# A graph network's second layer: one gather in sixty-four issued row by row by ScalarE

## The chip, the cores and the metric

The kernel runs on one core of a Trainium2 chip. A core has five engines that run their own instruction streams and meet at semaphores: TensorE (PE) multiplies matrices, VectorE (DVE) and ScalarE (ACT) do element work, GpSimd (POOL) does element work and also issues indirect transfers, and SyncE (SP) issues plain transfers. ScalarE can issue plain transfers too. The metric is the time of one execution on the device in microseconds (us), as the median of several runs.

## The reference

The graph has 12,500 nodes with 128 features and 400,000 edges, sorted by destination. Two layers follow each other. The first one (an edge network and a node network, each of two small matrix products) is not touched by the change. The second one, which is, computes

```python
# h = relu(layernorm(x)); 8 relations; W is 8 x 128 x 128, b is 8 x 128
H = jnp.einsum('ni,rio->rno', h, W)
msg = (H[etype, src] + b[etype]) * norm      # one row of 128 floats per edge
out = jax.ops.segment_sum(msg, dst, num_segments=h.shape[0])
x = x + relu(out)
```

So for each of the 400,000 edges one row of 512 bytes is fetched from a table with 12,500 x 8 rows, multiplied by the edge's weight, and added to the row of the edge's destination.

## The kernel before

**Tiling.** The edges are cut into tiles of 128 (`P`), eight tiles (`CT`) into a chunk of 1,024 edges, three chunks (`SC`) into a span. There are 391 chunks (`NC`) with 3,128 tiles. Within a chunk, the eight edges at one partition are neighbours in the sorted order, so that nearly all of the eight have the same destination.

**First layer.** A loop over the chunks fetches for each edge 32 floats of its source node by eight indirect transfers a chunk (line 358), runs the edge and node networks, and sums into windows of nodes. After each span it also computes the node rows of the second layer's table `tab_h` (8 relations x 128 floats per node, bias included). Beside the loop a generator, `prepare`, is advanced by one step per chunk. It turns indices and weights into the layouts that the second layer wants: it writes source times 8 plus type to a table `hidx_d` in HBM and loads it back, transposed, into `hidx_sb` (a column of 128 row numbers per tile). It has some 120 steps, and the loop has 390 turns.

**Second layer.** `layer1_once` is a loop over the chunks, fully unrolled. For one chunk:

- GpSimd issues eight indirect gathers (line 950). Each reads a column of `hidx_sb` and brings 128 rows of `tab_h` to the 128 partitions of `hg`, one slot of a tile of 8 x 128 floats. There are five buffers of `hg`.
- VectorE does this twice, for the two destinations that a partition can have (q = 0, 1): multiply `hg` by weights into `v` in PSUM (line 957), and sum `v` over the eight slots into `sm` (line 961).
- ScalarE casts `sm` to `hm` (line 964). This is its only instruction per chunk.
- One turn later (`sum_up`, called between the multiply and the sum of the next chunk) VectorE takes the rounding remainder (line 919), builds two one-hot matrices (line 921), and TensorE sums by destination into `acc` (line 924).
- Once per span SyncE reads the span's first node into a register (line 939), loads the window of nodes (lines 931 and 943), VectorE adds (lines 792 and 796), and SyncE writes back (lines 794 and 797).

**Order.** In the first layer the order of each engine's instructions is held to that of the source. The second layer stands in a conditional block; there the framework's scheduler orders each engine's stream. It also puts all semaphore waits in: all plain transfers, of SyncE and ScalarE together, take turns on eight completion semaphores, and each waits until the transfer before it on its semaphore has landed. The indirect transfers have eight others.

Of the kernel before, what the change touches and what calls it, by code (L numbers as in the profile page):

```python
# [8 lines left out]
F32 = mybir.dt.float32  # L9
F32R = mybir.dt.float32r  # L10
BF16 = mybir.dt.bfloat16
I32 = mybir.dt.int32
AF = mybir.ActivationFunctionType
OP = mybir.AluOpType
AX = mybir.AxisListType
ENG = mybir.EngineType
# [3 lines left out]
P = 128  # L20
D = 128
DE = 64
R = 8
N = 12500
# [5 lines left out]
CT = 8  # L30
# [4 lines left out]
NC = -(-E // CE)  # L35
# [8 lines left out]
T0 = 12 * CT  # L44
QT = 25 * 32
QS = 11
NONE = 16384

@with_exitstack
def gnn_kernel(  # L50
# [34 lines left out]
    nc = tc.nc  # L85
# [18 lines left out]
    const = ctx.enter_context(tc.tile_pool(name="const", bufs=1))  # L104
# [11 lines left out]
    span_d = dram.tile([1, NSP], F32, name="span_d")  # L116
    dst_d, hidx_d, ew_d = (dram.tile([NTP, P], F32, name=f"{name}_d") for name in ("dst", "hidx", "ew"))
    odd_d = dram.tile([1, P], F32, name="odd_d")


    ident = const.tile([P, P], F32, name="ident")
# [18 lines left out]
    hidx_sb = const.tile([P, NTP], I32, name="hidx_sb")  # L140
# [389 lines left out]
    with tc.tile_pool(name="e0", bufs=2) as pool, \  # L530
# [23 lines left out]
        def prepare():  # L554

            nc.sync.dma_start(w_f.rearrange("i (r o) -> i r o", r=R), w.rearrange("r i o -> i r o"))
            yield
            nc.sync.dma_start(b_f, b.to_broadcast([P, R * D]))
            yield
            for g in range(0, NTP, QT):  # L560
                m = min(QT, NTP - g)
                cols = slice(g, g + m)
                for given, table in ((dst_t, dst_d), (et, hidx_d), (ew, ew_d)):
                    raw = pool.tile([P, QT], F32, name="raw")
                    nc.sync.dma_start(raw[:, :m] if given is ew else raw[:, :m].bitcast(I32),
                                      given[:, cols])
                    yield
                    if given is dst_t:
                        nc.vector.tensor_copy(raw[:, :m], raw[:, :m].bitcast(I32))
                    elif given is et:  # L570
                        nc.vector.scalar_tensor_tensor(raw[:, :m], src_sb[:, cols], float(R),
                                                       raw[:, :m].bitcast(I32),
                                                       op0=OP.mult, op1=OP.add)
                    tr = pool.tile([P, QT], F32, name="tr")
                    nc.vector.transpose(tr[:, :m], raw[:, :m])
                    rows = table[cols, :].rearrange("(q r) (a j) -> a r q j", r=32, j=32)
                    for a in range(4):
                        nc.sync.dma_start(
                            rows[a], tr[32 * a:32 * a + 32, :m].rearrange("r (q j) -> r q j", j=32))
                    yield  # L580
            odd = pool.tile([P, NSP // QS], F32, name="odd", bufs=1)
            for i, s in enumerate(range(0, NSP, QS)):
                cols = slice(s * ST, (s + QS) * ST)
                hidx = pool.tile([P, QS * ST], F32, name="hidx")
                for table, to in ((dst_d, rel_t[:, cols]), (hidx_d, hidx), (ew_d, ew_sb[:, cols])):
                    nc.sync.dma_start(to.rearrange("p (c k) -> p c k", k=CT),
                                      table[cols, :].rearrange("(c t) (q k) -> (t q) c k",
                                                               t=CT, k=CT))
                    yield
                nc.vector.tensor_copy(hidx_sb[:, cols], hidx)  # L590
                rel = rel_t[:, cols]
                nc.vector.tensor_sub(rel.rearrange("p (s t) -> p s t", t=ST),
                                     rel.rearrange("p (s t) -> p s t", t=ST),
                                     base[:, s:s + QS, None].to_broadcast([P, QS, ST]))
                yield
                rel = rel.rearrange("p (c k) -> p c k", k=CT)
                off = []
                for k in (0, CT - 1):
                    o = pool.tile([P, QS * SC, CT], F32, name="off")
                    nc.vector.tensor_sub(o, rel,  # L600
                                         rel[:, :, k:k + 1].to_broadcast([P, QS * SC, CT]))
                    off.append(o)
                nc.vector.tensor_mul(off[0], off[0], off[1])
                nc.vector.tensor_mul(off[0], off[0], off[0])
                nc.vector.tensor_reduce(odd[:, i:i + 1], off[0].rearrange("p c k -> p (c k)"),
                                        AX.X, OP.max)
                yield
            most = pool.tile([P, 1], F32, name="most", bufs=1)
            nc.vector.tensor_reduce(most, odd, AX.X, OP.max)
            nc.sync.dma_start(odd_d.rearrange("o p -> p o"), most)  # L610
            yield
            odds = pool.tile([1, P], F32, name="odds", bufs=1)
            nc.sync.dma_start(odds, odd_d)
            yield
            nc.vector.tensor_reduce(vm[:, 1:2], odds, AX.X, OP.max)
            worst = pool.tile([1, 1], F32, name="worst", bufs=1)
            nc.vector.tensor_reduce(worst, vm, AX.X, OP.max)
            nc.vector.tensor_scalar(bad, worst, 0.0, None, op0=OP.is_gt)
            yield
            nc.sync.dma_start(x1_d[NP:NP + P, :], zeros[:, 0, :])  # L620
            yield from zero(zeros, agg_d)

        class Span:
# [16 lines left out]
            def end(self, left):  # L640

                a2 = add0(pool, self.aw, self.acc, P)
                if left:
                    nc.sync.dma_start(agg0_d[ds(self.row, P), :], a2)
                banks = ("u", "u", "u") if left else ("pre", "pm0", "pm1")
                steps = rows_h(pool, psum, self.row, self.x0, a2, banks)
                active.append(steps)
                if left:
                    node_step()
                else:  # L650
                    next(steps)
                    next(steps)
# [237 lines left out]
    def layer1_once():  # L890
# [3 lines left out]
        with tc.tile_pool(name="e1", bufs=2) as pool, \  # L894
# [33 lines left out]
            def write():  # L928
# [2 lines left out]
                nc.sync.dma_start(aw, agg_d[ds(row, P), :])  # L931
                return lambda: add_out(pool, aw, xw, (acc[:, 0:D], acc[:, D:2 * D]), row)

            for c in range(NC):
                s, k = divmod(c, SC)
                if k == 0:
                    if s % WS == 0:
                        w_p = weights(s)
                    row = nc.values_load(
                        span[0:1, s:s + 1], engines=[ENG.SP], min_val=0, max_val=N - 1,  # L940
                        skip_runtime_bounds_check_because="a span's least dst is a node")
                    xw = pool.tile([P, D], F32, name="xw1", bufs=3)
                    nc.sync.dma_start(xw, x1_d[ds(row, P), :])
                    acc = psum.tile([P, 512], F32, name="acc1", bufs=3)
                    sums_of.append((acc, row, xw))
                    if s:
                        end = write()
                hg = pool.tile([P, CT, D], F32, name="hg8", bufs=5)
                for t in range(c * CT, c * CT + CT):
                    nc.gpsimd.indirect_dma_start(  # L950
                        out=hg[:, t - c * CT, :], out_offset=None, in_=tab_hr,
                        in_offset=bass.IndirectOffsetOnAxis(ap=hidx_sb[:, t:t + 1], axis=0))
                sm = psum.tile([P, 2, D], F32, name="sm")
                t = c % (WS * SC) * CT
                for q in range(2):
                    v = psum.tile([P, CT, D], F32, name="v1", bufs=1)
                    nc.vector.tensor_tensor(  # L957
                        v, hg, w_p[:, q, t:t + CT, None].to_broadcast([P, CT, D]), op=OP.mult)
                    if todo:
                        sum_up(*todo.pop())  # L960
                    nc.vector.tensor_reduce(sm[:, q, :], v.rearrange("p t d -> p d t"),  # L961
                                            AX.X, OP.add)
                hm = pool.tile([P, 2, 2, D], F32R, name="hm2", bufs=6)
                nc.scalar.copy(hm[:, :, 0, :], sm)  # L964
                ends = rel_t[:, c * CT:c * CT + CT:CT - 1][:, :, None]
                todo.append((acc, sm, hm, ends, k == 0, k == SC - 1 or c == NC - 1))
                if k == SC - 1 and s:
                    end()
            sum_up(*todo.pop())
            for s in range((NC - 1) // SC - ((NC - 1) % SC < SC - 1), NS):  # L970
                if NC % SC and s < NS - 1:
# [73 lines left out]
```

## Time and profile before

| | us |
|---|---|
| median of three runs | 10107.48 (10087.31 to 10107.54) |
| the profiled execution, its own time | 7952.17 |
| its span, first to last instruction | 7950.4 |
| busy in the span: POOL | 5946.2 |
| busy: DVE | 5088.7 |
| busy: PE | 3303.0 |
| busy: ACT | 1627.5 |

The profiled execution is 2155 us shorter than the median of the runs, which the page doesn't explain. Everything in the profile is of that one execution. The second layer begins at about 4024 us of the span, and takes the remaining 3926 us. A line of the page that lists groups reads: source line, engine, operation, output<-input, count | busy time, mean ns of one | idle time just before them and what ended it. A page's "q" after an engine's name (SPq, ACTq) means its sequencer, which issues transfers and works on registers; these are not counted as busy time.

### The profile page before, as it was taken

Reading aid. Unit: us, or ns where it says so; the run is one execution under the profiler, and the core shown is the slowest. Engines: PE = TensorE matmul, PEld = TensorE weight load, DVE = VectorE, ACT = ScalarE, POOL = GpSimd, SP = SyncE. Lnnn points to the kernel's source line nnn. Section 1 sums busy time; section 2 is a strip of 40 time slices with the busy share of each in tenths; the row PEclk is TensorE's granted clock in tenths of the full one; section 3 lists DMA queues with packets and bytes.
Section 4 is the critical chain, followed back from the end, with each engine's and each line's share of the span. In section 5 each row is a group of like instructions: output and inputs, shape, how many; then the busy total and the mean of one; then the engine's idle time right before and its main releaser. Section 6 shows DMA issues by size and latency. Waiting matters only on the chain.

```text
span 7950.4 us, 66587 instructions
## 1 busy us (share of the span) xinstructions
PE 3303.0 (42%) x16589; PEld 1961.0 (25%) x16590; DVE 5088.7 (64%) x8155; ACT 1627.5 (20%) x3217; POOL 5946.2 (75%) x6273
## 2 busy tenths in 40 slices
PE   4877777777777777777710000000000000000000
PEld 3444444444444444444410000000000000000000
DVE  7887766666766766666655555555555555555555
ACT  3433333333333333333300000000000000000000
POOL 6777777777777777777757777777777777777776
PEclk7999899999999999989955555555555555555555
DMA  6655544333334333333322222222222222222222
GB/s 195 148 116 103 103 122 106 97 94 102 94 97 102 92 99 98 92 102 95 90 61 61 62 62 61 62 62 61 62 61 61 62 61 62 62 61 62 62 61 58
DMA packets 766351, 670.08 MB, mean 84 GB/s; under 512 B 382920, under 2 KB 587980, under 8 KB 765502
## 3 DMA queue, kind: packets, MB, share of 16 engines
q1 hardware_dynamic: 563608, 408.65, 17.9%
q0 software_dynamic: 200192, 256.65, 15.5%
q8 instruction: 135, 2.21, 0.1%
q14 instruction: 260, 2.13, 0.1%
q10 hardware_dynamic: 2156, 0.45, 0.0%
HBM read 526.07 MB, written 139.10 MB: 84 GB/s over the span
## 4 chain that ended last, share of the span: by engine, by line
POOL 56%; issue 24%; DMA 12%; DVE 5%; PE 1%; ACT 1%; SPq 0%; POOLq 0%; DVEq 0%; ACTq 0%
POOL hg L950 32%; POOL gb L358 24%; DMA gb<-tab_a,src_sb 9%; DMA hg<-tab_h,hidx_sb 3%; DVE nm L455 1%; DVE oh L460 1%; DVE ohT L383 1%; ACT nm L450 0%; DVE pq L449 0%; DVE ht L526 0%; DMA xt<-in_x 0%; DVE agT L403 0%; DVE z L405 0%; PE pq L441 0%; PE acc L465 0%
## 5 line engine op out<-in xcount | busy, mean ns | idle before, releaser
L950 POOL DMA_INDIRECT hg<-tab_h,hidx_sb x3128 | 2952.3, 944 | 997.3 <-issue 926.8
L358 POOL DMA_INDIRECT gb<-tab_a,src_sb x3032 | 2866.1, 945 | 925.6 <-issue 834.3
L957 DVE TENSOR_TENSOR v<-hg,io_p 128x1024 f32<-128x1024 f32 x782 | 959.7, 1227 | 1688.0 <-DMA hg<-tab_h,hidx_sb 1680.1
L924 PE MATMUL acc<-hm,oh 128*128 128x256 f32 x782 | 299.7, 484 | 3619.8 <-DVE oh L921 3586.8
L924 PEld LDWEIGHTS acc<-hm,oh 128*128 128x128 f32 x782 | 195.9, 311 | 3724.5 <-issue 3690.0
L961 DVE TENSOR_REDUCE sm<-v 128x128 f32<-128x1024 f32 x782 | 958.4, 1226 | 9.0
L964 ACT CAST hm<-sm 128x256 fp32r<-128x256 f32 x391 | 145.7, 373 | 3776.0 <-DVE sm L961 3776.0
L441 PE MATMUL pq<-w_n,h 128*128 128x256 f32 x3128 | 858.2, 424 | 0.0
L403 DVE STREAM_TRANSPOSE agT<-gb 128x256 f32<-128x256 f32 x391 | 173.5, 444 | 886.0 <-DMA gb<-tab_a,src_sb 883.8
L465 PE MATMUL acc<-nm,oh 128*128 128x256 f32 x3128 | 559.0, 328 | 390.8 <-DVE a L478 279.6
L441 PEld LDWEIGHTS pq<-w_n,h 128*128 128x128 f32 x3128 | 650.5, 218 | 90.8 <-issue 0.3
L465 PEld LDWEIGHTS acc<-nm,oh 128*128 128x128 f32 x3128 | 467.9, 219 | 556.1 <-issue 358.3
L450 ACT ACTIVATE nm<-pq 128x512 fp32r<-128x512 f32 x782 | 441.5, 597 | 602.9 <-DVE pq L449 601.0
L455 DVE SCALAR_TENSOR_TENSOR nm<-pq,nm 128x512 fp32r<-128x512 f32 x782 | 503.7, 686 | 71.9 <-ACT nm L450 27.7
L449 DVE TENSOR_TENSOR pq<-pq,b_n 128x512 f32<-128x512 f32 x782 | 504.8, 691 | 1.9 <-PE pq L441 1.9
L422 ACT ACTIVATE em<-pm,b_e 128x512 f32<-128x512 f32 x782 | 491.5, 681 | 65.2 <-PE pm L416 64.1
L434 ACT ACTIVATE h<-u,b_n 128x512 f32<-128x512 f32 x391 | 268.7, 687 | 1136.5 <-PE u L431 1127.5
L416 PE MATMUL pm<-h,w_e 64*128 64x256 f32 x3128 | 490.0, 436 | 2.5 <-ACT h L409 2.5
L383 DVE TENSOR_TENSOR ohT<-relb,io_p 126x1024 bf16<-126x1024 bf16 x391 | 473.1, 1210 | 15.8 <-DMA relb<-rel_d 15.7
L460 DVE TENSOR_TENSOR oh<-io_p,rel_s 128x1024 fp32r<-128x1024 f32 x391 | 475.7, 1217 | 0.0
L431 PE MATMUL u<-em,w_msg 128*64 128x512 f32 x1564 | 416.0, 599 | 7.0 <-ACT em L422 7.0
L525 PE MATMUL u<-w_f,hT 128*128 128x512 f32 x520 | 294.3, 648 | 209.6 <-ACT h L434 207.6
(117 smaller groups left out, 3220.5 us busy)
## 6 DMA issues: line engine op xcount, KB each, us to landing
eat<-in_ea SPq DMA_DIRECT2D x391, 256.0 KB
relb<-rel_d SPq DMA_DIRECT2D x391, 252.0 KB
tab_h<-ht SPq DMA_DIRECT2D x131, 512.0 KB
hg<-tab_h,hidx_sb POOLq DMA_INDIRECT x3128
gb<-tab_a,src_sb POOLq DMA_INDIRECT x3032
aw<-agg_d SPq DMA_DIRECT2D x262, 64.0 KB
agg_d<-a SPq DMA_DIRECT2D x261, 64.0 KB
agg_d<-zeros SPq DMA_DIRECT2D x48, 256.0 KB
```

The lines of the kernel that those rows point to most:

```text
L358: nc.gpsimd.indirect_dma_start(out=gb[:, t, :], out_offset=None, in_=tab_a, in_offset=bass.IndirectOffsetOnAxis(ap=idx(t), axis=0))
L383: nc.vector.tensor_tensor(self.ohT, self.relb, self.node.to_broadcast([WR, CE]), op=OP.is_equal)
L422: nc.scalar.activation(em, pms[h], AF.Relu, bias=b_e2)
L441: nc.tensor.matmul(pq[:, 2 * i:2 * i + 2, :], self.h2[:, P * (2 * k + i):P * (2 * k + i) + P], w_n2, start=True, stop=True)
L449: nc.vector.tensor_add(pq, pq, b_n2[:, None, :].to_broadcast([P, 4, D]))
L455: nc.vector.scalar_tensor_tensor(nm[:, :, 1, :], pq, 0.0, nm[:, :, 0, :], op0=OP.max, op1=OP.subtract)
L460: nc.vector.tensor_tensor(self.oh, self.iota[:, None, :].to_broadcast([P, CT, P]), rel[:, :, None].to_broadcast([P, CT, P]), op=OP.is_equal)
L465: nc.tensor.matmul(acc, self.oh[:, i, :], self.nm[:, i, :, :].rearrange("p q d -> p (q d)"), start=(start and i == 0), stop=(stop and i == ...
L924: nc.tensor.matmul(acc[:, 0:2 * D], oh[:, q, :], hm[:, q, :, :].rearrange("p r d -> p (r d)"), start=begin and q == 0, stop=stop and q == 1)
L950: nc.gpsimd.indirect_dma_start(out=hg[:, t - c * CT, :], out_offset=None, in_=tab_hr, in_offset=bass.IndirectOffsetOnAxis(ap=hidx_sb[:, t: ...
L957: nc.vector.tensor_tensor(v, hg, w_p[:, q, t:t + CT, None].to_broadcast([P, CT, D]), op=OP.mult)
L961: nc.vector.tensor_reduce(sm[:, q, :], v.rearrange("p t d -> p d t"), AX.X, OP.add)
```

## The change

In the second layer one tile of 128 rows in every eight chunks is no longer gathered by GpSimd. It is slot 7 (the eighth tile) of chunks 9, 17, 25 and so on to 385, 48 tiles in all. ScalarE fetches its 128 rows into a tile of its own, `hx7` (two buffers). It does this by 128 single transfers of one row (512 bytes), 16 in each of the eight chunks 8m to 8m+7, for use in chunk 8m+9. Before each 16 it loads their row numbers into 16 registers from `idx_scalar`, a tile of 48 x 128 integers. That tile is filled in `prepare` by one load from `hidx_d` and one conversion (two more steps). In a chunk with a fetched tile VectorE's multiply is split in two, one over slots 0 to 6 of `hg` and one over `hx7`.

```diff
+HELPERS = (("Activation", "scalar", 8, 7),)
...
+    helped = []
+    for name, queue, per, k in HELPERS:
+        n = (NC - 1 - per - 1) // per + 1
+        helped.append((getattr(ENG, name), getattr(nc, queue), per, k,
+                       const.tile([n, P], I32, name=f"idx_{queue}")))
...
+            by_chunk = hidx_d.rearrange("(c t) (q k) -> c (t q) k", t=CT, k=CT)
+            for _, _, per, k, to in helped:
+                n = to.shape[0]
+                rows = pool.tile([n, P], F32, name="rows", bufs=1)
+                nc.sync.dma_start(
+                    rows, by_chunk[per + 1:per + 2 + (n - 1) * per:per, :, k])
+                yield
+                nc.vector.tensor_copy(to, rows)
+                yield
...
+            def fetch(c):
+
+                for engine, queue, per, k, idx in helped:
+                    m, i = divmod(c, per)
+                    if m == idx.shape[0]:
+                        continue
+                    if i == 0:
+                        hx = pool.tile([P, D], F32, name=f"hx{k}", bufs=2)
+                        ahead.setdefault((m + 1) * per + 1, {})[k] = hx
+                    hx = ahead[(m + 1) * per + 1][k]
+                    at, end = i * P // per, (i + 1) * P // per
+                    _, rows = nc.values_load_multi_w_load_instructions(
+                        idx[m:m + 1, at:end], engines=[engine], min_val=0, max_val=N * R - 1,
+                        skip_runtime_bounds_check_because="src are nodes, and types relations")
+                    for p, row in zip(range(at, end), rows):
+                        queue.dma_start(hx[p:p + 1, :], tab_hr[ds(row, 1), :])
+
+            ahead = {}
             for c in range(NC):
...
                 hg = pool.tile([P, CT, D], F32, name="hg8", bufs=5)
-                for t in range(c * CT, c * CT + CT):
+                others = ahead.pop(c, {})
+                parts, at = [], 0
+                for t in range(CT):
+                    if t in others:
+                        parts += [(at, t, hg)] if at < t else []
+                        parts.append((t, t + 1, others[t]))
+                        at = t + 1
+                        continue
                     nc.gpsimd.indirect_dma_start(
-                        out=hg[:, t - c * CT, :], out_offset=None, in_=tab_hr,
-                        in_offset=bass.IndirectOffsetOnAxis(ap=hidx_sb[:, t:t + 1], axis=0))
+                        out=hg[:, t, :], out_offset=None, in_=tab_hr,
+                        in_offset=bass.IndirectOffsetOnAxis(
+                            ap=hidx_sb[:, c * CT + t:c * CT + t + 1], axis=0))
+                parts += [(at, CT, hg)] if at < CT else []
...
-                    nc.vector.tensor_tensor(
-                        v, hg, w_p[:, q, t:t + CT, None].to_broadcast([P, CT, D]), op=OP.mult)
+                    for a, b, rows in parts:
+                        nc.vector.tensor_tensor(
+                            v[:, a:b, :], rows[:, a:b, :] if rows is hg else rows[:, None, :],
+                            w_p[:, q, t + a:t + b, None].to_broadcast([P, b - a, D]), op=OP.mult)
...
                 todo.append((acc, sm, hm, ends, k == 0, k == SC - 1 or c == NC - 1))
                 if k == SC - 1 and s:
                     end()
+                fetch(c)
```

## The prediction

> **What bounds the kernel now.** I read the chain that ended last first, then the groups by line, then the timeline of a stretch in the second layer, then that of SyncE's transfers.
>
> ```profile
> span 7950.4 us, 66587 instructions
> POOL 56%; issue 24%; DMA 12%; DVE 5%; PE 1%; ACT 1%; SPq 0%; POOLq 0%; DVEq 0%; ACTq 0%
> L950 POOL DMA_INDIRECT hg<-tab_h,hidx_sb x3128 | 2952.3, 944 | 997.3 <-issue 926.8
> L358 POOL DMA_INDIRECT gb<-tab_a,src_sb x3032 | 2866.1, 945 | 925.6 <-issue 834.3
> L957 DVE TENSOR_TENSOR v<-hg,io_p 128x1024 f32<-128x1024 f32 x782 | 959.7, 1227 | 1688.0 <-DMA hg<-tab_h,hidx_sb 1680.1
> L964 ACT CAST hm<-sm 128x256 fp32r<-128x256 f32 x391 | 145.7, 373 | 3776.0 <-DVE sm L961 3776.0
> ```
>
> GpSimd is three quarters busy, and the rest of its time is "issue", a gap that waits for nothing the profile shows. VectorE waits for gathers (1680.1 us), ScalarE for VectorE (3776.0 of 3926 us). A stretch of the timeline shows the pace:
>
> ```profile
> 6002.50 0.94 POOL L950 DMA_INDIRECT hg<-tab_h,hidx_sb  x1 [0.30 <-issue]
> 6003.75 0.94 POOL L950 DMA_INDIRECT hg<-tab_h,hidx_sb  x1 [0.30 <-issue]
> 6005.00 0.94 POOL L950 DMA_INDIRECT hg<-tab_h,hidx_sb  x1 [0.30 <-issue]
> ...
> 6010.92 0.37 ACT L964 CAST hm<-sm 128x256 fp32r<-128x256 f32 x1 [9.70 <-DVE sm L961]
> ```
>
> A gather starts every 1.249 us, without exception; a chunk takes 8 x 1.249 = 9.99 us. The busy times by stretch agree (801 gathers in 1000 us) and show that the transfers' engines are only 24% busy there:
>
> ```profile
> 5000.00:6000.00 1000.00, 76.61 (x200) 50.08 (x200) 567.29 (x728) 37.25 (x100) 755.96 (x801) 0.50 0.24 62
> ```
>
> The columns are the stretch, its length, busy us (and instructions) of PE, weight loads, DVE, ACT and POOL, clock, DMA share, GB/s. VectorE has 5.7 us of work in each chunk of 10. GpSimd's pace is the bound, and in both layers: 6256 gathers x 1.249 = 7814 of 7950.4 us.
>
> **What the skill says.** "DMA: Bandwidth & Descriptors", section "Issuing engines are not separate DMA queues": transfers of all issuers run on the same 16 engines and interleave; another issuer only saves sequencer time. Here sequencer time is just what is short (gathers back to back, DMA share 0.24), so the trace agrees that a second issuer can help. "Runtime: NRT & Kernel Launch", section "Instruction fetch mechanics", puts a register load at about 200 ns per register, even in bulk. The trace has only loads of one register, 267 ns, and can't tell whether sixteen at once cost sixteen times that.
>
> **The change part by part.** *Removed*: 48 gathers x 1.249 = 60.0 us from GpSimd's stream, the bound.
>
> *Added on ScalarE*: per chunk 16 transfers with register addresses. The trace has no such row transfer on ScalarE; the nearest are SyncE's, whose registers also hold the address (128 rows of 512 bytes instead of one):
>
> ```profile
> 4007.57 0.33 SPq L510 DMA_DIRECT2D x_d<-x  x1
> 4008.10 0.33 SPq L511 DMA_DIRECT2D out<-x  x1
> 4008.62 0.35 SPq L472 DMA_DIRECT2D aw<-agg_d  x1
> ...
> L931 SPq FUSED_REGOPS  x131: 37/37/42, 4026.4 to 7940.4; - x131
> L931 SPq MOVE aw<-agg_d x131: 29/29/37, 4026.5 to 7940.5; - x131
> L931 SPq DMA_DIRECT2D aw<-agg_d x131: 333/354/360, 4026.6 to 7941.1; - x131
> ...
> L939 SPq TENSOR_LOAD <-span x131: 262/267/796, 4023.1 to 7879.8; - x131
> ...
> L272 ACTq DMA_DIRECT2D w_e<-in_we x4: 317/340/597, 10.1 to 24.2; - x4
> ```
>
> The last group is of ScalarE: its isolated issues take 317 to 340 ns like SyncE's, and up to 597 ns at the start of the kernel while SyncE loads large tiles. One register-addressed transfer every 0.53 us (4007.57, 4008.10, 4008.62) holds 37 + 29 ns of register work, 0.33 of issue and gaps. So 16 x 0.53 = 8.5 us a chunk, with 16 x 0.45 = 7.2 (no register work, gaps kept small) and 16 x 0.75 = 12.0 (0.60 issues plus the register work) as ends. The load of sixteen registers lies between 0.27 us (one instruction, flat) and 0.27 + 15 x 0.2 = 3.3 us (the skill's price). I take 1.0, nearer the flat end, since the sixteen words are neighbours and come in one instruction. The cast's 0.37 us runs on the engine while its sequencer issues; only the wait ahead of it, about 0.1 us, is in the stream. The sum is 8.5 + 1.0 + 0.1 = 9.6 us per chunk, with ends of 7.6 and 15.4.
>
> This is hidden as long as 384 chunks of it fit in GpSimd's new time, 3080 x 1.249 = 3847 us: up to 10.0 us per chunk. The cover is thin. What is queued behind the 16 rows is the next chunk's cast; if that is late, VectorE's `sum_up` of the chunk after waits, then `hg` comes free late. Five buffers of `hg` absorb a single delay, not a standing one.
>
> *Rows' landing*: the last of the 128 rows go out in the stretch after the cast of chunk 8m+7, and are read in chunk 8m+9; a gather's data is used some 3 us after its issue (6012.2 to 6015.16), so they arrive about when wanted. A few us late once in eight chunks fit in VectorE's 4.3 free us per chunk.
>
> *Semaphores*: rows and SyncE's four transfers per span take turns on eight. Eight rows take 4.2 us, more than the 3 us to land, so rows don't wait for each other. A row behind a write-back of SyncE (L794, L797) may wait some 2 to 3 us for it, once per span; SyncE's loads behind rows come up to a chunk later and have two chunks of slack.
>
> *VectorE*: 48 x 2 multiplies split in two. An eighth of the length moves to a second instruction; with a 128-wide operation at 0.28 us, 96 x (0.28 - 1.227/8) = 12 us, against its 1688 us of idle time. Nothing. *In `prepare`*: one small load and one conversion, two steps more for some 120 in 390 turns. Nothing, even in SyncE's queue.
>
> *Sum*: -60 us on the profiled 7952.17, i.e. 7892. The runs' median is 2155 us longer, and since GpSimd's pace makes up nearly all of the span, I assume that pace to be the difference: (10107.48 - 138) / 6256 = 1.594 us per gather, where 138 = 7952.17 - 6256 x 1.249. Then 48 gathers are 76 us: **10107.48 - 76 = 10031 us**. At that pace a chunk lasts 12.75 us and ScalarE's limit is 3080 x 1.594 / 384 = 12.8 us, if its issuing does not slow down too; if all slows alike, the margin is 9.6 against 10.0 times the same factor.
>
> **Rivals.** *ScalarE becomes the bound* (slower). From 10.0 us per chunk at the profile's pace: at 10.5 the second layer costs 384 x 10.5 - 3847 = 185 us over the new GpSimd time, so +125 net, x 1.27 = +159: 10266. At 11.9 (register load at the skill's price) 384 x 11.9 = 4570, +663 net, x 1.27 = 10950. For it: the thin cover, ScalarE's 0.6 us issues. Against it: idle engines at 24% and no large loads in that stage, and if only GpSimd is slower in the runs, the limit is 12.8. *The gathers slow down*: the row transfers come in between them on the engines and in HBM; 76 / 3080 = 25 ns more per gather, 1.6%, eats the gain, 50 ns give 10185. Against it: a gather's pace is the same to some ns whatever else runs. *A new wait takes the gain*: VectorE or SyncE held by rows in every span, 1.6 us in each of 48 helped chunks: 10107. Against it: the buffers and VectorE's slack.
>
> **How the numbers follow.** Gain as forecast, or with part of it lost to waits: 0.64. Wait takes the gain: 0.07. ScalarE the bound: 0.23. Gathers slower: 0.06. A measurement of this kernel can tell about 0.2% (20 us). The likeliest case alone spans 10015 (pace 1.6 and some ahead) to 10060 (the profile's pace and some waits, 10047 and up). Of the slower cases' 0.29, some half lie below 10420 (ScalarE up to about 11 us per chunk), so the range 10010 to 10420 leaves out some 0.15.
>
> **What would show it.** Right: 3080 gathers at L950's successor still 1.25 us apart; ScalarE with 6144 transfers some 0.53 us apart, its register loads near 1 us, and still a wait of the cast for `sm`; VectorE still waiting for gathers. Wrong: the cast no longer waits for `sm`, VectorE's remainder (L919) waits for the cast, GpSimd waits for `hg` buffers; then ScalarE is the bound, and its row spacing or register load says which price was wrong. A gather spacing above 1.27 us would mean contention.

## The result, and the profile after

| | before | after |
|---|---|---|
| median of the runs, us | 10105.69 (10087.31 to 10107.54, 4 runs) | 11191.87 (11185.89 to 11239.84, 4 runs) |
| span of the profiled execution, us | 7950.4 | 11184.1 |

The ratio is 1.109 (95% interval 1.1057 to 1.1123): the change makes the kernel 1086 us slower. One thing has to be known to read these numbers: on two of the four chips that the runs below fell on, the kernel before takes about 7960 us, on the other two 10090 to 10221 us, and the first profile of before was taken in the first condition while the timed runs, and the profile of after, were in the second. On which chip these first ones fell isn't on record, so whether a chip can change its condition isn't known. The two are called the 7960 condition and the 10100 condition here, and every run is compared with runs of before on its own chip.

The page of after has these groups, lines renumbered (L991 is the gather, L1009 ScalarE's cast, L935 VectorE's remainder):

```profile
span 11184.1 us, 85299 instructions
L991 POOL DMA_INDIRECT hg<-tab_h,hidx_sb x3080 | 2913.2, 946 | 2683.1 <-DVE v L1001 882.1
L935 DVE TENSOR_TENSOR hm<-sm,hm 128x256 fp32r<-128x256 f32 x391 | 165.7, 424 | 3075.6 <-ACT hm L1009 2711.7
L1009 ACT CAST hm<-sm 128x256 fp32r<-128x256 f32 x391 | 145.6, 372 | 5309.5 <-DMA hx<-tab_h 4448.4
```

Before, the gathers' idle time was 997.3 us, nearly all of it "issue"; now it is 2683.1, most of it for VectorE. Before, the cast waited for VectorE's `sm`; now 4448.4 us of its wait end with a transfer of `hx`. The table of waits for 6000 to 11000 us of after (engine, line, waited for: us in total, times, longest) has the whole chain:

```profile
ACT hm L1009 <- DMA hx<-tab_h: 4187.7, 308, 30.4
DVE hm L935 <- ACT hm L1009: 2502.8, 238, 21.9
POOL hg L991 <- DVE v L1001: 814.3, 102, 17.3
POOL hg L991 <- DVE a L808: 667.1, 74, 17.3
```

ScalarE's cast stands behind its row transfers, VectorE behind the cast, GpSimd behind VectorE for a free `hg`. These are the three signs that the prediction named for "ScalarE is the bound". The timeline of ScalarE in after shows what its sequencer does (start, us, line, operation, count):

```profile
8001.07 8.05 ACTq L965 DMA_DIRECT2D hx<-tab_h  x16
8009.23 0.37 ACT L1009 CAST hm<-sm 128x256 fp32r<-128x256 f32 x1 [9.23 <-DMA hx<-tab_h]
8010.72 6.26 ACTq L965 DMA_DIRECT2D hx<-tab_h  x16
8017.10 0.37 ACT L1009 CAST hm<-sm 128x256 fp32r<-128x256 f32 x1 [7.49 <-DMA hx<-tab_h]
8018.54 26.06 ACTq L965 DMA_DIRECT2D hx<-tab_h  x15
8046.08 0.37 ACT L1009 CAST hm<-sm 128x256 fp32r<-128x256 f32 x1 [28.61 <-DMA hx<-tab_h]
```

Sixteen rows take 6.26 us in one chunk and 26.06 in the next (of those sixteen the trace has fifteen). Over the layer, casts are 13.92 us apart on average, and ScalarE's sequencer is hardly ever free: a cast follows the last row ahead of it within 0.2 us on average, so its `sm` is nearly always there already. What fills the long chunks is seen in the groups of single instructions, here of 6500 to 7700 us of after (count: shortest/median/longest ns):

```profile
L965 ACTq DMA_DIRECT2D hx<-tab_h x1388: 1/223/1394, 6500.0 to 7697.1; - x199
L965 ACTq FUSED_REGOPS  x1388: 1/37/1405, 6500.5 to 7698.5; - x199
L965 ACTq MOVE hx<-tab_h x1388: 1/29/1402, 6500.5 to 7699.2; - x199
```

The median of each is short. But some instructions, register operations too, take 0.70 or 1.40 us. They come in stretches: of the 51 steps of a chunk, 43 take 5.5 us together, and some 8 that are 0.64 to 1.6 us long, the register load among them, take 7.5. Steps of over 1.6 us, where a row waits for a semaphore, are only 0.8 us per chunk. The work by 1000 us of the second layer is (PE, weight loads, DVE, ACT, POOL; then clock, DMA share, GB/s)

```profile
7000.00:8000.00 1000.00, 56.98 (x144) 36.05 (x144) 421.84 (x543) 27.19 (x73) 540.84 (x573) 0.50 0.17 45
```

573 instructions of GpSimd where the 7960 condition had 801 before, and idle transfer engines: not a contention for bandwidth.

### The profile page after: what moved, and what is told of

Its sections match the earlier page's. It is cut to its first block, busy times and chain, and to the rows that moved or that the text cites. A ratio compares the mean times of both kernels' runs of the same rounds, so it can differ in the third digit from the quotient of the medians.

```text
span 11184.1 us, 85299 instructions
## 1 busy us (share of the span) xinstructions
PE 3770.0 (34%) x16589; PEld 1988.2 (18%) x16590; DVE 5200.0 (46%) x8252; ACT 1609.2 (14%) x3217; POOL 5909.1 (53%) x6225
## 3 DMA queue, kind: packets, MB, share of 16 engines
q1 hardware_dynamic: 569768, 408.67, 12.8%
## 5 line engine op out<-in xcount | busy, mean ns | idle before, releaser
L991 POOL DMA_INDIRECT hg<-tab_h,hidx_sb x3080 | 2913.2, 946 | 2683.1 <-DVE v L1001 882.1
L935 DVE TENSOR_TENSOR hm<-sm,hm 128x256 fp32r<-128x256 f32 x391 | 165.7, 424 | 3075.6 <-ACT hm L1009 2711.7
L438 PE MATMUL u<-em,w_msg 128*64 128x512 f32 x1564 | 721.7, 710 | 928.8 <-ACT em L429 707.2
L1001 DVE TENSOR_TENSOR v<-hg,io_p 128x1024 f32<-128x1024 f32 (+1 forms) x782 | 946.5, 1210 | 44.6 <-DMA hg<-tab_h,hidx_sb 25.2
L1009 ACT CAST hm<-sm 128x256 fp32r<-128x256 f32 x391 | 145.6, 372 | 5309.5 <-DMA hx<-tab_h 4448.4
L448 PE MATMUL pq<-w_n,h 128*128 128x256 f32 x3128 | 751.5, 383 | 0.0
L532 PE MATMUL u<-w_f,hT 128*128 128x512 f32 x520 | 404.5, 870 | 680.8 <-ACT h L441 625.1
L423 PE MATMUL pm<-h,w_e 64*128 64x256 f32 x3128 | 573.1, 497 | 57.5 <-ACT h L441 41.3
L448 PEld LDWEIGHTS pq<-w_n,h 128*128 128x128 f32 x3128 | 576.4, 194 | 65.7 <-issue 0.7
L472 PE MATMUL acc<-nm,oh 128*128 128x256 f32 x3128 | 509.6, 309 | 33.0 <-DVE a L485 15.7
L472 PEld LDWEIGHTS acc<-nm,oh 128*128 128x128 f32 x3128 | 428.2, 204 | 200.6 <-issue 124.5
```

What stands on the lines that cost most here:

```text
L423: nc.tensor.matmul(pms[h][:, 256 * i:256 * i + 256], w_e2[rows, 2 * h + i, :], self.h1[rows, :], start=True, stop=True)
L438: nc.tensor.matmul(u[64 * h:64 * h + 64, :], w_msg, self.em[h], start=False, stop=True)
L448: nc.tensor.matmul(pq[:, 2 * i:2 * i + 2, :], self.h2[:, P * (2 * k + i):P * (2 * k + i) + P], w_n2, start=True, stop=True)
L472: nc.tensor.matmul(acc, self.oh[:, i, :], self.nm[:, i, :, :].rearrange("p q d -> p (q d)"), start=(start and i == 0), stop=(stop and i == ...
L991: nc.gpsimd.indirect_dma_start(out=hg[:, t, :], out_offset=None, in_=tab_hr, in_offset=bass.IndirectOffsetOnAxis(ap=hidx_sb[:, c * CT + t: ...
L1001: nc.vector.tensor_tensor(v[:, a:b, :], rows[:, a:b, :] if rows is hg else rows[:, None, :], w_p[:, q, t + a:t + b, None].to_broadcast([P, ...
```

## The experiments

Theories, by their letters: **P**, in the 10100 condition GpSimd's gather pace is slower (the prediction's assumption); **A**, ScalarE's stream is too full as such (A1, A2, B and C are variants, told apart in single runs); **S**, the condition of the chip decides. Later: **R**, in the 10100 condition every instruction of a sequencer costs a share of a common limit; **T**, row transfers cost, not instructions; **E**, each engine's own stream is held up. The expectations speak of chips by number: 1 and 15 were in the 7960 condition, 0 and 14 in the other.

### Four kernels in the 7960 condition

The kernel before here took 7966.23 us (21 runs). First the kernel before once more, as a yardstick.

> The kernel before, unchanged, for a second profile. The first one's span was 7950 us where the runs' median is 10106. Theory S (the sequencers have stretches in which every one of their instructions takes about 0.70 us; the first profile had none, most executions have them): a span of about 10100, such stretches on SyncE, a first layer near the 5650 us that it takes in the profile of after, a second layer of about 4450, and gathers still 1.25 us apart wherever GpSimd does not wait. Theory P (what the prediction assumed: a gather has a slower pace in the usual executions): gathers 1.59 us apart in both layers and no such stretches.

7966.66 us, ratio 1.0001 (0.9991 to 1.0011). Its trace has gathers at 1.25 us and nothing like after's stretches.

The second leaves out the row transfers and the register loads; the tile is zeroed, so its output lacks those rows.

```diff
                     if i == 0:
                         hx = pool.tile([P, D], F32, name=f"hx{k}", bufs=2)
+                        nc.vector.memset(hx, 0.0)
...
-                    for p, row in zip(range(at, end), rows):
-                        queue.dma_start(hx[p:p + 1, :], tab_hr[ds(row, 1), :])
```

> The change without ScalarE's register loads and row transfers: the 48 tiles stay out of GpSimd's stream, and hx7 is filled with zeros by VectorE instead (the output lacks these rows). It shows what the removed gathers are worth alone. Theory A (ScalarE's stream of rows is the whole cost): 60 to 76 us less than before, so about 10030 to 10045. Theory B (something else in the change costs, the split multiply or the new order of the streams): clearly above 10106.

7905.94 us, ratio 0.9926 (0.9904 to 0.9949): -60.3 us. The 48 gathers are worth 48 x 1.249 = 60.0 us, as the first step of the prediction had it.

The third fetches the rows and doesn't use them; all 3128 gathers stay.

```diff
-                others = ahead.pop(c, {})
+                ahead.pop(c, {})
+                others = {}
```

> The change with all 3128 gathers kept on GpSimd and VectorE's multiply whole: ScalarE fetches the 48 tiles, and nobody reads them. It shows the cost of the row stream alone, without a wait of VectorE for the rows. Theory A (the casts stand behind 16 rows in ScalarE's stream, 13.7 us per chunk): as slow as the change, 11150 to 11300. Theory C (VectorE's wait for the rows' landing is what costs): near 10106 plus at most 100.

7967.09 us, ratio 1.0002 (0.9992 to 1.0012). Here 6144 rows on ScalarE cost nothing. Theory A falls for this condition.

The fourth has SyncE issue the rows.

```diff
-HELPERS = (("Activation", "scalar", 8, 7),)
+HELPERS = (("SP", "sync", 8, 7),)
```

> The same 128 row transfers per tile, issued by SyncE in place of ScalarE, so that no cast stands behind a row. Theory A1 (it is the place ahead of the casts that costs): the casts are free, rows have 8 chunks of time, SyncE needs up to 13.7 us per chunk of 12.7: at or below 10300. Theory A2 (a sequencer can't issue 16 rows in a chunk's time, whatever else stands in its stream): rows come late to the helped chunks, second layer again about 5400 us, total 11000 to 11400.

7907.94 us, ratio 0.9928 (0.9906 to 0.9951): -58.3 us. Another issuer does as well.

### Three kernels in the 10100 condition

The kernel before here took 10221.27 us. The first is the change as it is. The second adds SyncE as a further helper with slot 6 (96 tiles in all), the third has one tile in sixteen chunks (24 tiles, 8 rows a chunk; the expectation's 23 is a miscount).

```diff
-HELPERS = (("Activation", "scalar", 8, 7),)
+HELPERS = (("Activation", "scalar", 8, 7), ("SP", "sync", 8, 6))
```
```diff
-HELPERS = (("Activation", "scalar", 8, 7),)
+HELPERS = (("Activation", "scalar", 16, 7),)
```

> The change, unchanged, a second time, beside the kernel before on the same chip. In the group of runs before this one the kernel before took 7966 us, the rows alone cost nothing and 48 gathers less gave 60 us. Theory S (the loss of 1086 us belongs to executions in which sequencers have stretches of about 0.70 us per instruction): if the kernel before takes about 7966 here, the change takes 7900 to 7915, with rows 0.39 us apart and no such stretches; if the kernel before takes about 10106 here, the change takes about 11190. Theory A (ScalarE's stream is too full as such): 11190 or, beside a before of 7966, at least 8700.

> A second tile (slot 6) of the helped chunks fetched by SyncE in the same way, beside ScalarE's slot 7: 96 gathers leave GpSimd's stream. Theory S, beside a before of 7966: another 60 us off, 7840 to 7860; beside a before of 10106: slower than the change or equal, since both sequencers issue 16 rows a chunk. Theory A: no faster than the change.

> Half the rows: one tile in every sixteen chunks, 8 rows per chunk on ScalarE, 23 tiles. Theory S, beside a before of 7966: 23 x 1.25 = 29 us off, about 7937. Beside a before of 10106: ScalarE's stream, 13.7 us per chunk with 16 rows, falls to about 7 and is hidden again, so about 10070.

11412.72, 12759.32 and 10674.53 us: ratios 1.1164 (1.113 to 1.1197), 1.2481 (1.2427 to 1.2535) and 1.0442 (1.0408 to 1.0475). The loss is the condition's, so S stands. But half the rows were expected to hide again, and still cost 453 us: casts were 12.38 us apart with 8 rows a chunk, which undisturbed would be about 4 us of work (an estimate: 8 rows at the 0.394 us that a row takes in the other condition, below, and a load). The stream isn't merely a little too long.

### What is held up: four kernels in the 10100 condition

The kernel before here took 10090.24 us (13 runs). First that kernel again, for the profile that was missing.

> The kernel before, unchanged, for a profile on the chip of this job. Two conditions have been seen: the kernel before at 7966 (chip 1), and at 10106 to 10221 (elsewhere). Where it is at about 10200 here, theory R (in that condition every engine's sequencer has stretches in which an instruction takes 0.70 us, whatever is run) expects a span of about 10150 to 10200, layer 1 near 5700 instead of 4020 and layer 2 near 4150 to 4300, and register operations and moves of 0.70 us on SyncE in the trace. A theory that only the change brings such stretches expects none in this trace. Where it is at 7966, the trace repeats the first one.

10095.45 us, ratio 1.0008 (0.9998 to 1.0018). SyncE's load of a window in the second layer, from the trace of before in the 7960 condition (5900 to 9900 us):

```profile
L931 SPq FUSED_REGOPS  x69: 37/37/42, 5901.6 to 7940.4; - x69
L931 SPq DMA_DIRECT2D aw<-agg_d x69: 354/354/360, 5901.7 to 7941.1; - x69
```

and of the same kernel in the 10100 condition:

```profile
L931 SPq FUSED_REGOPS  x119: 688/698/709, 5911.9 to 9876.7; - x119
L931 SPq DMA_DIRECT2D aw<-agg_d x119: 689/699/714, 5914.0 to 9878.8; - x119
```

The 0.70 us are there without the change. A register operation of 37 ns takes 698, each time. The gathers of this trace in the second layer, and its work from 7000 to 8000 us in the columns used above:

```profile
L950 POOL DMA_INDIRECT hg<-tab_h,hidx_sb x2857: 942/949/1936, 6000.2 to 9998.6; - x191
7000.00:8000.00 1000.00, 68.23 (x178) 44.63 (x178) 505.99 (x650) 33.19 (x89) 765.55 (x716) 0.50 0.21 55
```

Their median is 949 ns, as before, but some last up to 1936. They start 1.394 us apart on average, so a chunk takes 11.15 us. The first layer is stretched far more: from the start of the kernel to the first cast of the second layer it is 5698 us against 4043. Of the 2112 us between the two spans 1656 lie there, and there most gathers still follow each other at 1.25 us, with gaps of 5 us and more between chunks. So P falls: the gap between the two conditions is not one pace of gathers.

Next, the kernel without rows again (the diff is that of the second kernel above).

> No row transfers and no register loads: 48 gathers are left out and the tile of 128 rows is zeroed by VectorE instead (the output lacks those rows). On chip 1 this gave -60. Beside a before of about 10200: my prediction's pace for that condition, 1.594 us per gather, expects -76; if GpSimd's gathers in layer 2 hold 1.25 us there too, -60; if in that condition VectorE or another engine bounds the layer, about 0. In all these cases the loss of 1190 is then entirely the price of ScalarE's stream.

10038.12 us, ratio 0.9947 (0.9917 to 0.9976): -52 us, within -24 to -84. The removed gathers are worth about the same in both conditions. The loss of the change is therefore all the price of its rows: 1080 + 52 = 1132 us.

Next, the change with fixed addresses.

```diff
-                    _, rows = nc.values_load_multi_w_load_instructions(
-                        idx[m:m + 1, at:end], engines=[engine], min_val=0, max_val=N * R - 1,
-                        skip_runtime_bounds_check_because="src are nodes, and types relations")
-                    for p, row in zip(range(at, end), rows):
-                        queue.dma_start(hx[p:p + 1, :], tab_hr[ds(row, 1), :])
+                    for p in range(at, end):
+                        row = 2053 * m + 17 * p
+                        queue.dma_start(hx[p:p + 1, :], tab_hr[row:row + 1, :])
```

> The change with its 16 row transfers per chunk on ScalarE at fixed addresses: no register load and no register operations, so 1 sequencer instruction per row instead of 3 (the rows fetched are others than wanted, and the output differs). Theory R (each instruction of the sequencer is held up in the slow condition): beside a before of about 10200 the loss falls from 1190 to about a third or less, so under 450, and ScalarE's rows take about 5 to 8 us per chunk instead of 14. Theory T (what is held up is the transfer, 0.19 us per row whatever issues it): the loss stays at 1000 to 1200. Beside a before of 7966 both expect what the removed gathers give, 7907 (-60).

10289.53 us, ratio 1.0197 (1.0159 to 1.0234): +199 us instead of +1080 to +1190, with just as many transfers. T falls. Casts are 11.69 us apart instead of 13.92.

Last, the kernel before with 32 copies of one element on ScalarE per chunk, in a small tile `idle` of their own.

```diff
...
                 if k == SC - 1 and s:
                     end()
+                for i in range(32 if c < 384 else 0):
+                    nc.scalar.copy(idle[0:1, 1:2], idle[0:1, 0:1])
```

> The kernel before, all its gathers kept, with 32 copies of one element on ScalarE after each of 384 casts: 12288 more instructions on ScalarE, none of them a transfer or a register operation. About 0.2 us each, 6.4 us per chunk, so where nothing stalls they are hidden: 7966 beside 7966. Beside a before of about 10200: theory R, if any instruction counts, +0.07 us each, so about +600 to +900; theory T, and a form of R in which only register operations and transfer issues are held up, within 40 us of before.

10828.54 us, ratio 1.0731 (1.0695 to 1.0767): +738 us, without one transfer or register operation added. Undisturbed, 32 copies at 0.22 us and the cast would be some 7.5 us of the 10.0 (an estimate from the trace below). The timeline of ScalarE:

```profile
8000.28 6.42 ACT L972 COPY idle<-idle 1x1 f32<-1x1 f32 x29
8006.60 0.36 ACT L966 CAST hm<-sm 128x256 fp32r<-128x256 f32 x1
8006.87 1.52 ACT L972 COPY idle<-idle 1x1 f32<-1x1 f32 x7
...
8013.16 0.19 ACT L972 COPY idle<-idle 1x1 f32<-1x1 f32 x1 [0.52 <-ACT idle L972]
8014.55 0.19 ACT L972 COPY idle<-idle 1x1 f32<-1x1 f32 x1 [1.20 <-ACT idle L972]
8015.95 0.19 ACT L972 COPY idle<-idle 1x1 f32<-1x1 f32 x1 [1.21 <-ACT idle L972]
8017.36 0.19 ACT L972 COPY idle<-idle 1x1 f32<-1x1 f32 x1 [1.22 <-ACT idle L972]
```

This is the clearest sight of it. A copy lasts 0.19 us throughout, and 29 of them follow each other in 6.42 us; then, for some 20 us, one starts every 0.70 or 1.40 us. The operation isn't slower; the engine gets its next instruction late. The end of the same timeline shows two things more:

```profile
10711.19 0.36 ACT L966 CAST hm<-sm 128x256 fp32r<-128x256 f32 x1
10711.46 105.84 ACT L972 COPY idle<-idle 1x1 f32<-1x1 f32 x476
```

The scheduler left 476 copies behind the last cast. So some 88 of the 738 us are this tail (107 us from the last cast to the end, where before has 19 in this condition), and not time lost within the chunks. And the tail runs at 0.22 us per copy without one delay: the last gather was issued at 10682.67 us, and none of the some 600 copies after it starts late, where until then a stretch of late ones had begun every 38 us or so.

### Whose limit it is: three kernels in the 10100 condition

The kernel before here took 10100.1 us. The first adds 16 matmuls of one column per chunk on TensorE, into an unused half of `sm`'s bank; for that, `sm` becomes a part of a larger tile, which the matmuls write too.

```diff
-                sm = psum.tile([P, 2, D], F32, name="sm")
+                sp = psum.tile([P, 4, D], F32, name="sm")
+                sm = sp[:, 0:2, :]
...
+                for i in range(16 if c < 384 else 0):
+                    nc.tensor.matmul(sp[0:1, 3, 0:1], ident[:, 0:1], ident[:, 0:1],
+                                     start=True, stop=True)
```

> The kernel before, all its gathers kept, with 16 matmuls of one column into an unused part of a PSUM tile on TensorE for each of 384 chunks: 32 or more instructions in the record per chunk (12288 in all, more if a matmul is split), on an engine that is idle for nine tenths of the second layer. No ScalarE instruction is added. Where nothing is held up they are hidden: 7966 beside 7966. Beside a before of about 10100: theory R with a limit shared by all engines expects about +0.06 to 0.07 us per added instruction, so +700 to +900 for 12288; a limit that each engine has for itself (theory E: ScalarE's own stream is slow, TensorE has room) expects within 100 us of before.

10730.82 us, ratio 1.0623 (1.0566 to 1.068): +631 us. Each matmul became two, with a weight load each, so 24,959 instructions more are on the page. That is 0.025 us each, not 0.06 to 0.07; but casts are 12.75 us apart, though neither ScalarE nor VectorE nor GpSimd has an instruction more. The waits (6500 to 10500 us) have a new line for VectorE's remainder, whose other side this view can't name:

```profile
DVE hm L919 <- remote: 2170.8, 312, 12.7
```

The semaphores of the same trace name it. VectorE waits there for the one that the last of the chunk's added matmuls raises, since the remainder reads the tile that they write; in 95 of 100 chunks it goes on within 0.03 us of that. The semaphore is raised 3.1 us after the end that the profile models for the last matmul where it is early, 5.9 in the median, and 11.0 or more in one chunk of ten. So this kernel put TensorE's own stream into the chain of every chunk, where it was meant to be idle, and it is TensorE that comes late. (How long it takes undisturbed isn't known: this kernel, like that with the copies, did not run in the 7960 condition.)

The second is the kernel with SyncE as the issuer, which in the other condition gained 58 us.

> The change with its rows issued by SyncE instead of ScalarE, as before on chip 1 (-58). Beside a before of about 10100: theory R, shared limit, expects the same loss as with ScalarE, +1000 to +1200, since the number of instructions is the same; theory E with ScalarE alone slow expects a gain of about 50. Beside a before of 7966 it repeats the -58.

12404.55 us, ratio 1.228 (1.2245 to 1.2316): +2304 us, twice what the same rows cost on ScalarE. SyncE's timeline:

```profile
9016.54 12.53 SPq L965 DMA_DIRECT2D hx<-tab_h  x16
9030.16 0.36 SPq L977 DMA_DIRECT2D xw<-x_d  x1
9030.73 0.36 SPq L947 DMA_DIRECT2D aw<-agg_d  x1
9032.33 14.41 SPq L965 DMA_DIRECT2D hx<-tab_h  x32
```

SyncE is now the full stream, 17.1 us of steps per chunk and as much between casts, with the windows' loads and write-backs queued among the rows. Theory R in its shared form falls with these two runs, by the price of one added instruction:

| kernel, against which | us more | instructions more | us each |
|---|---|---|---|
| fixed addresses on ScalarE, no rows | 251 | 5,928 | 0.042 |
| copies on ScalarE, before | 738 | 12,290 | 0.060 |
| the change (below), no rows | 1132 | 18,614 | 0.061 |
| matmuls on TensorE, before | 631 | 24,959 | 0.025 |
| rows on SyncE, no rows | 2356 | 18,914 | 0.125 |

(Instructions are the counts at the top of the pages; "no rows" is taken as 52 us under before. Without their tail the copies cost 650 us, 0.053 each.) A limit that charges every instruction the same would give one price. And with helpers on both engines the loss was 2538 us, near that of SyncE alone and far from the sum of 1080 and 2304. What fits all the runs is E in a wider form than its text gave it: each engine's own stream is held up, and the chunk takes as long as the most loaded one that it has to wait for. This is argued from the prices, and doesn't say where the hold-ups come from.

The traces do say when they come. Counted are register operations and moves, undisturbed 37 and 29 ns long, that last over 0.5 us, by the time since the latest gather, of either layer, began:

| trace, sequencer | within 1.3 us of a gather's start | over 5 us after it |
|---|---|---|
| before, 10100 condition, SyncE | 1097 of 2335 | 6 of 651 |
| the change (profile of after), ScalarE | 988 of 7602 | 4 of 3182 |
| rows on SyncE, 10100 condition, SyncE | 1826 of 5288 | 81 of 9759 |

In the 7960 condition there is none among the 3404 of before nor the 15,694 of the change, gathers or not. So in the 10100 condition sequencers are held up while GpSimd issues gathers, and run freely again a few microseconds after it stops; the copies' tail fits. That gathers hold them up isn't proved by this, since when GpSimd waits most other engines wait too, and no run takes the gathers away.

The third kernel is the change again.

> The change as it is. Beside a before of about 10100 a loss of 1090 to 1190, as twice before. Beside a before of 7966 the prediction's own mechanism is tested for the first time on the condition of its profile: 16 rows at 0.39 us and a load of 1.2 us are 7.5 us of ScalarE per chunk, under 10.0, so GpSimd stays the bound and the time falls by 58 to 60, to about 7907. If ScalarE's stream fills as it did with all gathers kept (9.7 us per chunk), the limit is near and the gain is smaller, down to nothing.

11179.78 us, ratio 1.1068 (1.1036 to 1.11): +1080 us, the chip's condition again deciding.

### The change in the 7960 condition

The last two fell on a chip where the kernel before takes 7953.57 us (19 runs). One is the change as it is, the other has a quarter of its tiles (12, with 4 rows per chunk).

```diff
-HELPERS = (("Activation", "scalar", 8, 7),)
+HELPERS = (("Activation", "scalar", 32, 7),)
```

> The change as it is, in the hope of the other condition. Beside a before of 7966: ScalarE's stream of 16 rows and a load takes 7.9 us per chunk, under 10.0, and the time falls by 58 to 60, to about 7907. Beside a before of about 10100: +1080 to +1190, as three times before, with ScalarE's stream at 13.9 us per chunk.

> The change with 12 tiles fetched by ScalarE instead of 48, each over 32 chunks, so 4 rows and one load per chunk. Beside a before of 7966: 12 gathers fewer, -15. Beside a before of about 10100: if the stream's length grows with its instructions (13.9 us for 16 rows, 12.4 for 8, so about 11.6 for 4, against 11.15 us per chunk that GpSimd takes there), +100 to +200; if a stretched stream still hides as long as it is short (theory: only a full stream loses), -13.

The change: 7892.00 us, ratio 0.9923 (0.9894 to 0.9952), -61.6 us. A quarter of it: 7939.80 us, ratio 0.9983 (0.9976 to 0.9991), -13.8 us, where 12 x 1.249 = 15. What so short a stream costs in the 10100 condition was not seen, and no version that keeps the output gained in both conditions. The change's page and ScalarE's timeline here:

```profile
span 7890.5 us, 85299 instructions
L991 POOL DMA_INDIRECT hg<-tab_h,hidx_sb x3080 | 2906.7, 944 | 982.5 <-issue 902.2
```
```profile
7010.15 6.65 ACTq L965 DMA_DIRECT2D hx<-tab_h  x16
7016.92 0.37 ACT L1009 CAST hm<-sm 128x256 fp32r<-128x256 f32 x1 [7.81 <-DMA hx<-tab_h]
7018.34 6.37 ACTq L965 DMA_DIRECT2D hx<-tab_h  x16
7024.83 0.37 ACT L1009 CAST hm<-sm 128x256 fp32r<-128x256 f32 x1 [7.54 <-DMA hx<-tab_h]
7026.25 12.71 ACTq L965 DMA_DIRECT2D hx<-tab_h  x16
```

The same instructions as in after, and GpSimd's idle time is "issue" again. A chunk of ScalarE's takes 7.9 us, and every third one some 6 us more: a row stands still until about 3 us after SyncE has issued the write-back of the span, which comes before it on their semaphore. So ScalarE fills the 9.84 us between casts, but some 2 us of each are this wait, whose end GpSimd's pace sets through the sums; the bound is GpSimd.

## Why the prediction was wrong, step by step

**Removed gathers, 60.0 us.** Right: -61.6 with the change and -60.3 without rows. The sum against the profiled execution, "i.e. 7892", is what the change takes in that condition, 7892.00; that it fits to the microsecond is luck, since the kernel before took 7953.57 there. For the timed runs the prediction had 76 us; the gathers' removal alone gave 52 in their condition (24 to 84).

**ScalarE's stream, 9.6 us per chunk with ends of 7.6 and 15.4.** Its sum was too high by a fifth without disturbance, 9.6 against 7.9: a row every 0.394 us instead of 0.53 (0.230 for the issue, where 128 rows took 0.33 to 0.36), but a register load of 1.20 us instead of 1.0. And even there the cast had no wait for `sm` left, against the prediction's sign of being right: of the idle time ahead of it (L1009, 4500 to 7800 us) 3081.9 us end with a transfer of `hx`. The Trainium skill ("Runtime: NRT & Kernel Launch", "Instruction fetch mechanics") has about 200 ns per register; sixteen at once took 1.18 to 1.25 us, so 75 ns each, and the measurement decides. In the 10100 condition the stream is 13.9 us. The end of 15.4 takes that in, but for prices of rows and loads that were not what happened.

**Semaphores.** "A row behind a write-back of SyncE (L794, L797) may wait some 2 to 3 us for it": 6 us on average, once per span. Hidden, as said.

**The step that failed** is the last of the sum: "since GpSimd's pace makes up nearly all of the span, I assume that pace to be the difference: ... 1.594 us per gather", and with it the limit of "12.8 us, if its issuing does not slow down too; if all slows alike, the margin is 9.6 against 10.0 times the same factor". The runs showed neither. Gathers of the second layer went from 1.249 to 1.394 us apart, a factor of 1.12, and ScalarE's stream from 7.9 us undisturbed to 13.9, a factor of 1.76. GpSimd has one gather per 1.25 us and lost little; ScalarE has 51 steps per chunk, most of them under 0.1 us undisturbed, and a step that is held up costs it 0.70 or 1.40 us. The cost that the sum had wrong is thus ScalarE's stream, 9.6 us per chunk on paper and 13.9 in the runs. The limit was 10.97 us (the casts' distance without rows in that condition), not 12.8, so 2.95 us were missing per chunk; from the 11.14 of before (on another chip of that condition) to 13.92 it is 2.78 x 390 = 1084 of the 1086 us.

**The rival "ScalarE becomes the bound"** had the right mechanism, place and signs, at a chance of 0.23; its dearest case, 11.9 us per chunk, gave 10950, and the range stopped at 10420. It was sized from the first profile's prices of single instructions, and that profile was of an execution in which the cause doesn't occur. That the profile and the runs differed by 2155 us was seen and put into a factor instead of into the range.

**"Issuing engines are not separate DMA queues"** (the Trainium skill, "DMA: Bandwidth & Descriptors") says that another issuer only saves sequencer time. The traces agree, at a DMA share of 0.17 to 0.24; but sequencer time was short on the new issuer too.

**What stays open.** What it is about the time of the gathers that holds up the sequencers in the 10100 condition, and why it doesn't in the other, isn't settled. Fetching instructions over the transfer queues doesn't look slower: their blocks of 8 KB took a median of 0.44 us in the trace of before in that condition and 0.40 in the other; whether they are asked for late isn't seen. The traces of that condition also hold only a quarter to a third of the semaphore records (35,969 updates against 157,382 for the same kernel), so something in reporting events is different there too; whether it is cause or companion no run tells.

## What to carry to other kernels

Where the profiled execution and the timed runs differ by more than their scatter, the profile is of another state: find out which engine's steps the gap lies in before it is spread over one pace, and widen the range until both readings fit. Before moving work to an idle engine count the instructions that replace one, not their busy time alone: here 392 short steps (8 chunks of 49) stand in place of one gather, free in one condition and 1132 us in all in the other. An idle engine is not a free one if its next necessary instruction, here a cast of 0.37 us, queues behind the new ones.

## What the runs showed of the hardware

- In one condition of the chip, sequencer steps on SyncE and ScalarE become 0.70 or 1.40 us long, in stretches of some 10 to 25 us and more; a register operation of 37 ns then takes 698. Compute instructions start late in the same way while lasting as long as ever (copies of 0.19 us).
- In that condition nearly all late steps fall into the time of the gathers: of SyncE's register operations in the kernel before, 1097 of 2335 within 1.3 us of a gather's start lasted over 0.5 us, and 6 of 651 more than 5 us after it.
- The same 48 tiles on the same engine: -61.6 us in one condition, +1080 to +1191 in the other. On SyncE: -58 and +2304.
- One row of 512 bytes with its address in a register every 0.394 us on ScalarE (37 and 29 ns of register work, 230 of issue), where 128 rows had 0.33 to 0.36 of issue; sixteen registers loaded in 1.20 us.
- All plain transfers sharing eight completion semaphores, a row of ScalarE stood about 6 us behind SyncE's write-back, once per span.
